# Attention scores of two layers in smaller TensorE tiles: layer 0 from 64x128 to 64x64, layer 3 from 32x128 to 32x64

## The chip, the cores and the metric

One core of a Trainium2 chip runs the whole program. The metric is the device time of one execution in microseconds (us); lower is better. A run is called faster or slower only beyond 2%. All runs told here were in the fast state.

A few names, as the profile uses them: PE is TensorE's matmuls, PEld its weight loads, ACT is ScalarE, DVE is VectorE. L1321 is line 1321 of that kernel; after an edit the same statement has another number. A tile of 32x128 (32\*128 in the profile) is a part of TensorE's array, 32 rows by 128 columns; several tiles work side by side as a pack (the first passes of layer 3's four start within 20 ns, and one record reads 640 ns), and the shape of the tile is the tile mode. A matmul in float32 leaves two records in the trace, its first and its second pass (the 1024 matmuls of L1008 leave 2048). A weight load is exposed when TensorE has nothing to stream meanwhile. In a group's row, what stands between the bars is its busy us and the mean ns of one record; after the second bar comes its engine's idle time before it and what ended that. A row of a timeline starts with its start and its length in us. A semaphore event is the record by which the trace tells that something another engine waits for is done.

## The reference, cut to what matters

Four layers work on x of 4 images, 64 x 64 tokens, 64 channels, all in float32. Layers 0, 2 and 3 are attentions; layer 1 is a convolution block with 1x1 projections.

```python
# layer 0: per image, 4096 tokens of 64 channels
energy = jnp.einsum('bic,bjc->bij', q, k)
attn = jax.nn.softmax(energy, axis=-1)
out = jnp.einsum('bmn,bmc->bnc', attn, v)
# ... layer 1 (convolution block), layer 2 (attention of 64x64) cut
# layer 3: per image, 4096 tokens of 32 channels
f = jnp.einsum('bnd,bmd->bnm', theta_x, phi_x)
f = jax.nn.softmax(f, axis=-1)
y = jnp.einsum('bnm,bmd->bnd', f, g_x)
```

## The kernel before

The scores are built in PSUM buffers called `ps` (128x1024 each, three buffers). ScalarE takes the exponential of a whole `ps` into an SBUF tile `e`, and TensorE multiplies `e` with the values. Scores of one step, products of an earlier step and, in layers 0 and 2, pieces of the convolution block are issued in a fixed order. That a matmul behind a waiting one waits too is what experiment 4 shows: there the second of a set starts 0.191 us after the first, because it waits, and the third 7 ns behind the second.

```python
def new_ps(name="ps"):                                  # pool of 3 buffers
    return pp.tile([128, 1024], F32, tag="ps", name=name)

# layer 0: contraction over 64 channels, two row tiles side by side
for g in range(4):
    ps = new_ps()
    for r in range(2):
        rows_ = slice(64 * r, 64 * r + 64)
        mm(ps[:, bass.ts(r, 512)], m.q[rows_, bass.ts(t, 128)],
           x[rows_, bass.ts(g, 512)], start=True, stop=True)
    act(es[g // 2][:, bass.ts(g % 2, 1024)], ps, AF.Exp, bias=SHIFT0,
        accum_out=zs[:, g : g + 1])

# a projection of the convolution block: the same shape, 64 rows and 128 columns
for s in range(2):
    mm(ps[:, bass.ts(s, 512)], pw1[64 * s : 64 * s + 64, bass.ts(r, 128)],
       tok(y, s, j), start=True, stop=True)

# layer 3: contraction over 32 channels, four row tiles, two ps for a step
e = es[n] = new_e()
tiles = [new_ps(), new_ps()]
for k in range(4):
    rows_ = slice(32 * k, 32 * k + 32)
    mm(tiles[k // 2][:, bass.ts(k % 2, 512)], m.ph[rows_, bass.ts(mc, 128)],
       m.th[rows_, bass.ts(nb, 512)], start=True, stop=True)
for kp in range(2):
    act(e[:, bass.ts(kp, 1024)], tiles[kp], AF.Exp)
# ... products of step n - 2 follow; in about every tenth step also sums by matmul
```

Of the kernel before, what the change touches and what calls it, by code (L numbers as in the profile page):

```python
# [691 lines left out]
def fast_path(ctx: ExitStack, tc: tile.TileContext, a: dict, out: bass.AP, bad):  # L692
# [18 lines left out]
    def new_ps(name="ps"):  # L711
        return pp.tile([128, 1024], F32, tag="ps", name=name)

    def new_acc(name="acc"):
        return pa.tile([128, 512], F32, tag="acc", name=name)

    def new_e(name="e"):
        return ep.tile([128, 2048], F32, tag="e", name=name)

    def new_t(name="t"):  # L720
        return tp.tile([128, 1024], F32, tag="t", name=name)
# [7 lines left out]
    mm = nc.tensor.matmul  # L729
# [73 lines left out]
    for nm in names128:  # L803
        r = flat[nm].shape[0] // 128
# [126 lines left out]
    def at(i, fn):  # L931
        due.setdefault(i, []).append(fn)
# [63 lines left out]
    def layer0(b):  # L996
        x, m, first = X[:, b], im[b], len(items)
        tiles = {}

        def scores(t):  # L1000
            es = [new_e() for _ in range(2)]
            zs = sm.tile([128, 4], F32, tag="zs", name="zs", bufs=4)
            vq = sm.tile([128, C], F32, tag="vq", name="vq", bufs=4)
            for g in range(4):
                ps = new_ps()
                for r in range(2):
                    rows_ = slice(64 * r, 64 * r + 64)
                    mm(  # L1008
                        ps[:, bass.ts(r, 512)], m.q[rows_, bass.ts(t, 128)],
                        x[rows_, bass.ts(g, 512)], start=True, stop=True,  # L1010
                    )
                act(  # L1012
                    es[g // 2][:, bass.ts(g % 2, 1024)], ps, AF.Exp, bias=SHIFT0,
                    accum_out=zs[:, g : g + 1],
                )
            tiles[t] = es, vq, zs

        def scale(t):
            es, vq, zs = tiles[t]
            tot = sums0[:, b, t : t + 1]  # L1020
            nc.vector.tensor_reduce(tot, zs, AX.X, ALU.add)
            rec = sm.tile([128, 1], F32, tag="rec", name="rec")
            nc.vector.reciprocal(rec, tot)
            nc.vector.tensor_scalar_mul(vq, m.v[:, t, :], rec)

        def products(p, half):
            accs = [new_acc() for _ in range(2)]
            for t in (2 * p, 2 * p + 1):
                es, vq, _ = tiles[t]
                for g in range(2):  # L1030
                    for r in range(2):
                        mm(  # L1032
                            accs[g][64 * r : 64 * r + 64, :], vq,
                            es[half][:, 1024 * g + 512 * r : 1024 * g + 512 * r + 512],
                            start=t == 2 * p, stop=t == 2 * p + 1,
                        )
            for g in range(2):
                cols = bass.ts(2 * half + g, 512)
                stt(  # L1039
                    (x if p == 15 else m.y)[:, cols], accs[g], gam0,  # L1040
                    (m.y if p else x)[:, cols], ALU.mult, ALU.add,
                )

        for t in range(32):
            items.append((lambda t=t: scores(t), 3.6))
        for p in range(16):
            for half in range(2):
                at(first + 2 * p + 2 + half, lambda p=p, half=half: products(p, half))
        for t in range(32):
            at(first + t, lambda t=t: scale(t))  # L1050
# [260 lines left out]
    def layer3(b):  # L1311
        m, first, last = im[b], len(items), b == B - 1
        es, st = {}, {}

        def scores(n):
            nb, mc = n // 32, n % 32
            e = es[n] = new_e()
            tiles = [new_ps(), new_ps()]
            for k in range(4):
                rows_ = slice(32 * k, 32 * k + 32)  # L1320
                mm(  # L1321
                    tiles[k // 2][:, bass.ts(k % 2, 512)], m.ph[rows_, bass.ts(mc, 128)],
                    m.th[rows_, bass.ts(nb, 512)], start=True, stop=True,
                )
            for kp in range(2):
                act(e[:, bass.ts(kp, 1024)], tiles[kp], AF.Exp)  # L1326

# [86 lines left out]
        for n in range(64):  # L1414
            items.append((lambda n=n: scores(n), 1.0))
            at(first + n + 2, lambda n=n: products(n))
            if last and n == 63:
                at(first + n + 2, close_last)
            elif n % 32 == 31:
                at(first + n + (2 if n == 63 and b < 2 else 4), lambda n=n: totals(n // 32))  # L1420
                at(first + n + 8, lambda n=n: close(n // 32))
# [69 lines left out]
    ps = new_ps()  # L1491
# [13 lines left out]
    for b in range(B):  # L1505
        dst = out[b].rearrange(by_rows, p=2, q=16)
        for g in range(2):
# [9 lines left out]
            ps = new_ps()  # L1517
# [23 lines left out]
    for i, (v, lo, hi) in enumerate(vals):  # L1541
        n = v.shape[1]
        total += 128 * n
        t = new_t("inside")
        nc.vector.tensor_scalar(t[:, 0:n], v, lo, None, ALU.is_ge)
        stt(t[:, 0:n], v, hi, t[:, 0:n], ALU.is_le, ALU.mult, accum_out=good[:, i : i + 1])
    ps = new_ps()
# [52 lines left out]
```

## Time and profile before

| | before |
|---|---|
| median of 3 runs (a fourth came with the result) | 2722.68 us (2719.42 to 2723.97) |
| span of the profiled run | 2718.6 us |
| granted TensorE clock | 0.994 |
| instructions in the trace | 41825 |
| layer 3, from its first to its last score group, three stretches | 146.8 + 146.6 + 304.3 = 597.7 us |

Layer 3's images 0 and 1 stand each in a stretch of their own, images 2 and 3 follow one another in the third. The lines that carry the reading are in the prediction below. Read them for one thing above all: a busy TensorE tells nothing about the short gaps in which it loads weights (534 against 429 ns from the first to the second pass in layer 0's scores) or changes its tile mode (519 against 422 ns from the last record of one group to the first of the next). For those one needs the starts of single records.

### The profile page before, as it was taken

Reading aid. Unit: us, or ns where it says so; the run is one execution under the profiler, and the core shown is the slowest. Engines: PE = TensorE matmul, PEld = TensorE weight load, DVE = VectorE, ACT = ScalarE, POOL = GpSimd, SP = SyncE. Lnnn points to the kernel's source line nnn. Section 1 sums busy time; section 2 is a strip of 40 time slices with the busy share of each in tenths; the row PEclk is TensorE's granted clock in tenths of the full one; section 3 lists DMA queues with packets and bytes.
Section 4 is the critical chain, followed back from the end, with each engine's and each line's share of the span. In section 5 each row is a group of like instructions: output and inputs, shape, how many; then the busy total and the mean of one; then the engine's idle time right before and its main releaser. Section 6 shows DMA issues by size and latency. Waiting matters only on the chain.

```text
span 2718.6 us, 41825 instructions
## 1 busy us (share of the span) xinstructions
PE 2656.8 (98%) x18042; PEld 902.6 (33%) x18042; DVE 1349.0 (50%) x1507; ACT 1724.6 (63%) x2796; POOL 16.6 (1%) x66
## 2 busy tenths in 40 slices
PE   8999999999999999999999999999999999999996
PEld 3343333333333333323333332243322333322222
DVE  3232478437773478216720027920058700088888
ACT  4545655565556555555655668855678756578886
POOL 2000000000000000000000000000000000000000
PEclk9999999999999999999999999999999999999998
DMA  3000000000000000000010000010000010010001
GB/s 71 0 1 1 1 1 1 1 1 1 1 1 1 8 8 1 1 1 17 1 32 1 16 1 1 1 32 1 17 1 1 1 32 1 1 32 1 1 1 64
DMA packets 17349, 24.33 MB, mean 9 GB/s; under 512 B 2460, under 2 KB 10885, under 8 KB 17157
## 3 DMA queue, kind: packets, MB, share of 16 engines
q1 hardware_dynamic: 16085, 20.47, 3.1%
q8 instruction: 143, 2.34, 0.4%
q0 software_dynamic: 672, 0.56, 0.1%
q10 hardware_dynamic: 400, 0.56, 0.1%
q14 instruction: 49, 0.40, 0.0%
HBM read 4.80 MB, written 4.19 MB: 3 GB/s over the span
## 4 chain that ended last, share of the span: by engine, by line
PE 94%; DVE 4%; ACT 2%; issue 0%; DMA 0%; ACTq 0%; DVEq 0%
PE acc L1032 17%; PE ps L1008 17%; PE acc L1224 16%; PE ps L1207 16%; PE ps L1321 11%; PE acc L1348 9%; PE ps L1103 1%; PE ps L1160 1%; PE accz L1337 1%; PE ps L1078 1%; PE ps L1143 1%; PE ps L1171 1%; PE ps L1064 1%; PE ps L1302 1%; PE ps L985 1%; DVE tg L1344 0%
## 5 line engine op out<-in xcount | busy, mean ns | idle before, releaser
L1012 ACT ACTIVATE e<-ps 128x1024 f32<-128x1024 f32 x512 | 517.1, 1024 | 343.4 <-PE ps L1008 231.0
L1215 ACT ACTIVATE e<-ps 128x1024 f32<-128x1024 f32 x512 | 517.1, 1024 | 308.1 <-PE ps L1207 308.0
L1326 ACT ACTIVATE e<-ps 128x1024 f32<-128x1024 f32 x512 | 495.4, 1022 | 94.9 <-PE ps L1321 85.1
L1344 DVE TENSOR_TENSOR tg<-tg,e 128x2048 f32<-128x2048 f32 x214 | 490.4, 2292 | 26.1 <-ACT e L1326 7.4
L1008 PE MATMUL ps<-X,q 64*128 64x512 f32 x2048 | 482.7, 608 | 11.3 <-ACT e L1012 4.2
L1207 PE MATMUL ps<-ko 64*64 64x512 f32 x4096 | 470.4, 593 | 7.8 <-ACT ko L1189 5.5
L1224 PE MATMUL acc<-e,X 64*64 64x512 f32 x4096 | 468.0, 591 | 2.7 <-DVE X L1039 2.1
L1032 PE MATMUL acc<-e,vq 128*64 128x512 f32 x2048 | 468.4, 599 | 0.0
L1321 PE MATMUL ps<-tg,ph 32*128 32x512 f32 x2048 | 321.2, 640 | 0.5 <-ACT e L1326 0.5
L1039 DVE SCALAR_TENSOR_TENSOR yv<-acc,gam,yv 128x512 f32<-128x512 f32 x224 | 168.0, 750 | 290.4 <-PE acc L1032 278.6
L1008 PEld LDWEIGHTS ps<-X,q 64*128 64x128 f32 x2048 | 187.0, 187 | 295.3 <-issue 190.1
L1348 PE MATMUL acc<-e,tg 128*32 128x512 f32 x2048 | 272.0, 603 | 1.3 <-ACT yz L1354 1.3
L1207 PEld LDWEIGHTS ps<-ko 64*64 64x64 f32 x4096 | 156.4, 133 | 294.7 <-issue 196.4
L1224 PEld LDWEIGHTS acc<-e,X 64*64 64x64 f32 x4096 | 159.6, 133 | 280.3 <-issue 265.0
L1032 PEld LDWEIGHTS acc<-e,vq 128*64 128x64 f32 x2048 | 136.6, 137 | 311.7 <-issue 290.3
L1232 DVE TENSOR_TENSOR ph<-ph,acc 128x512 f32<-128x512 f32 x16 | 11.0, 688 | 423.7 <-ACT ph L1231 423.7
L1321 PEld LDWEIGHTS ps<-tg,ph 32*128 32x128 f32 x2048 | 103.2, 182 | 219.2 <-issue 139.9
L1125 DVE SCALAR_TENSOR_TENSOR yg<-pad,vec,yg 128x1024 f32<-128x1024 f32 x128 | 164.3, 1283 | 5.9 <-ACT pad L1108 2.4
L1125 DVE SCALAR_TENSOR_TENSOR y<-pad,vec,y 128x1024 f32<-128x1024 f32 x128 | 164.3, 1284 | 3.7
L1348 PEld LDWEIGHTS acc<-e,tg 128*32 128x32 f32 x2048 | 43.5, 108 | 190.6 <-issue 185.1
L1215 ACT ACTIVATION_READ_ACCUMULATOR e<-ps 128x1 f32 x512 | 106.0, 207 | 0.0
L1012 ACT ACTIVATION_READ_ACCUMULATOR e<-ps 128x1 f32 x512 | 106.0, 207 | 0.0
(187 smaller groups left out, 996.5 us busy)
## 6 DMA issues: line engine op xcount, KB each, us to landing
ph<-tg SPq DMA_DIRECT2D x64, 128.0 KB
ko<-ko SPq DMA_DIRECT2D x16, 256.0 KB
out_dram<-o SPq DMA_DIRECT2D x8, 512.0 KB
xr<-in_x_dram SPq DMA_DIRECT2D x14, 256.0 KB
xr<-in_x_dram ACTq DMA_DIRECT2D x2, 256.0 KB
pw<-in_L_conv_pw_w_dram POOLq DMA_DIRECT2D x4, 64.0 KB, 4.6
sca<-in_L_conv_sca_w_dram POOLq DMA_DIRECT2D x1, 64.0 KB, 6.2
pw<-in_L_conv_pw_w_dram POOLq DMA_DIRECT2D x2, 32.0 KB, 4.8
```

Of the source, the lines that this page charges most:

```text
L1008: mm(ps[:, bass.ts(r, 512)], m.q[rows_, bass.ts(t, 128)], x[rows_, bass.ts(g, 512)], start=True, stop=True,)
L1012: act(es[g // 2][:, bass.ts(g % 2, 1024)], ps, AF.Exp, bias=SHIFT0, accum_out=zs[:, g : g + 1],)
L1032: mm(accs[g][64 * r : 64 * r + 64, :], vq, es[half][:, 1024 * g + 512 * r : 1024 * g + 512 * r + 512], start=t == 2 * p, stop=t == 2 * p + 1,)
L1039: stt((x if p == 15 else m.y)[:, cols], accs[g], gam0, (m.y if p else x)[:, cols], ALU.mult, ALU.add,)
L1125: stt(out_, win, wt, out_, ALU.mult, ALU.add)
L1207: mm(ps[64 * c : 64 * c + 64, bass.ts(r, 512)], m.ko[rows_, 128 * jb + 64 * c : 128 * jb + 64 * c + 64], m.ko[rows_, bass.ts(2 * ib + r, 5 ...
L1215: act(es[n, jb], ps, AF.Exp, bias=SHIFT2, accum_out=m.zs[:, jb, ib : ib + 1])
L1224: mm(acc[r][64 * c : 64 * c + 64, :], xw[rows_, jb, :], es[n, jb][rows_, bass.ts(c, 512)], start=jb == 0, stop=jb == 31,)
L1321: mm(tiles[k // 2][:, bass.ts(k % 2, 512)], m.ph[rows_, bass.ts(mc, 128)], m.th[rows_, bass.ts(nb, 512)], start=True, stop=True,)
L1326: act(e[:, bass.ts(kp, 1024)], tiles[kp], AF.Exp)
L1344: nc.vector.tensor_add(esum, esum, e)
L1348: mm(st["y"][32 * k : 32 * k + 32, :], m.gx[:, mc, :], e[:, bass.ts(k, 512)], start=mc == 0, stop=mc == 31,)
```

## The change

The intent: tiles of 64 columns instead of 128 load their weights faster (133 against 187 ns for a record; where the load is exposed, it costs 51 against 105 ns), so less of the load is exposed where it can't be hidden.

```diff
@@ layer 0
-                for r in range(2):
-                    rows_ = slice(64 * r, 64 * r + 64)
-                    mm(
-                        ps[:, bass.ts(r, 512)], m.q[rows_, bass.ts(t, 128)],
-                        x[rows_, bass.ts(g, 512)], start=True, stop=True,
-                    )
+                for c in range(2):
+                    for r in range(2):
+                        rows_ = slice(64 * r, 64 * r + 64)
+                        mm(
+                            ps[64 * c : 64 * c + 64, bass.ts(r, 512)],
+                            m.q[rows_, 128 * t + 64 * c : 128 * t + 64 * c + 64],
+                            x[rows_, bass.ts(g, 512)], start=True, stop=True,
+                        )
@@ layer 3
-            for k in range(4):
-                rows_ = slice(32 * k, 32 * k + 32)
-                mm(
-                    tiles[k // 2][:, bass.ts(k % 2, 512)], m.ph[rows_, bass.ts(mc, 128)],
-                    m.th[rows_, bass.ts(nb, 512)], start=True, stop=True,
-                )
+            for c in range(2):
+                for k in range(4):
+                    rows_ = slice(32 * k, 32 * k + 32)
+                    mm(
+                        tiles[k // 2][64 * c : 64 * c + 64, bass.ts(k % 2, 512)],
+                        m.ph[rows_, 128 * mc + 64 * c : 128 * mc + 64 * c + 64],
+                        m.th[rows_, bass.ts(nb, 512)], start=True, stop=True,
+                    )
```

## The prediction

Two measurements from the trace of the kernel before, to be kept in mind while reading: the matmuls of a pack start 6.7 ns apart (the four of a layer 3 set that doesn't wait at 0, 7, 13 and 20 ns), and in the 166 of layer 3's 256 score sets in which the third matmul waited, the fourth started 6 or 7 ns behind it.

> **What bounds the kernel now.** I read the page first, then the groups by line, then the timeline of a stretch of layer 3, then single records of the trace there. The page:
>
> ```profile
> PE 2656.8 (98%) x18042; PEld 902.6 (33%) x18042; DVE 1349.0 (50%) x1507; ACT 1724.6 (63%) x2796; POOL 16.6 (1%) x66
> ...
> PE 94%; DVE 4%; ACT 2%; issue 0%; DMA 0%; ACTq 0%; DVEq 0%
> PE acc L1032 17%; PE ps L1008 17%; PE acc L1224 16%; PE ps L1207 16%; PE ps L1321 11%; PE acc L1348 9%; PE ps L1103 1%; PE ps L1160 1%; PE accz L1337 1%; PE ps L1078 1%; PE ps L1143 1%; PE ps L1171 1%; PE ps L1064 1%; PE ps L1302 1%; PE ps L985 1%; DVE tg L1344 0%
> ```
>
> TensorE is busy 98% of the span and makes 94% of the chain that ended last. But busy is the union of overlapping records[...]. The chain's lines are the score and product matmuls of the three attention layers; the change touches L1008 (layer 0) and L1321 (layer 3). The groups:
>
> ```profile
> L1326 ACT ACTIVATE e<-ps 128x1024 f32<-128x1024 f32 x512 | 495.4, 1022 | 94.9 <-PE ps L1321 85.1
> ...
> L1008 PE MATMUL ps<-X,q 64*128 64x512 f32 x2048 | 482.7, 608 | 11.3 <-ACT e L1012 4.2
> L1207 PE MATMUL ps<-ko 64*64 64x512 f32 x4096 | 470.4, 593 | 7.8 <-ACT ko L1189 5.5
> L1321 PE MATMUL ps<-tg,ph 32*128 32x512 f32 x2048 | 321.2, 640 | 0.5 <-ACT e L1326 0.5
> ...
> L1008 PEld LDWEIGHTS ps<-X,q 64*128 64x128 f32 x2048 | 187.0, 187 | 295.3 <-issue 190.1
> L1207 PEld LDWEIGHTS ps<-ko 64*64 64x64 f32 x4096 | 156.4, 133 | 294.7 <-issue 196.4
> L1321 PEld LDWEIGHTS ps<-tg,ph 32*128 32x128 f32 x2048 | 103.2, 182 | 219.2 <-issue 139.9
> ```
>
> Each f32 matmul is two records (1024 instructions of L1008 give 2048). A load of 128 columns reads 187 ns, of 64 columns 133 ns. Layer 2 (L1207) already has the 64*64 tiles that layer 0 is to get. Now layer 3 in order of time, near its last image:
>
> ```profile
> 2592.80 0.37 PEld L1321 LDWEIGHTS ps<-tg,ph 32*128 32x128 f32 x8 [0.84 <-issue]
> 2592.80 1.20 PE L1321 MATMUL ps<-tg,ph 32*128 32x512 f32 x8
> 2593.93 0.16 PEld L1348 LDWEIGHTS acc<-e,tg 128*32 128x32 f32 x8 [0.76 <-issue]
> 2593.93 1.06 PE L1348 MATMUL acc<-e,tg 128*32 128x512 f32 x8
> 2593.97 1.94 ACT L1326 ACTIVATE e<-ps 128x1024 f32<-128x1024 f32 x2 [0.24 <-PE ps L1321]
> 2594.93 0.42 PEld L1321 LDWEIGHTS ps<-tg,ph 32*128 32x128 f32 x8 [0.84 <-issue]
> 2594.93 1.25 PE L1321 MATMUL ps<-tg,ph 32*128 32x512 f32 x8
> 2596.10 1.94 ACT L1326 ACTIVATE e<-ps 128x1024 f32<-128x1024 f32 x2 [0.19 <-PE ps L1321]
> 2596.11 0.16 PEld L1348 LDWEIGHTS acc<-e,tg 128*32 128x32 f32 x8 [0.76 <-issue]
> 2596.11 1.06 PE L1348 MATMUL acc<-e,tg 128*32 128x512 f32 x8
> 2597.10 0.37 PEld L1321 LDWEIGHTS ps<-tg,ph 32*128 32x128 f32 x8 [0.84 <-issue]
> ```
>
> One step of layer 3 is one group of scores, one of products and two exponentials. It starts at 2592.80, 2594.93, 2597.10: 2.13 and 2.17 us. ScalarE is busy 1.94 us of it, then waits about 0.2 us for the scores. So neither engine alone sets the pace: they pass it to and fro through the three `ps` buffers. That coupling is what the prediction turns on.
>
> [...] from the last record of one group to the first of the next is 517 to 523 ns whenever the mode changes (64*128 to 128*64, 64*64 to 128*64, 32*128 to 128*32, all alike) and 422 (two tiles) or 409 (four tiles) where it stays; about 97 ns a change. [...] a group whose weights could not be fetched during the one before it takes 534 ns from first to second pass with 128 columns, 480 with 64, against 429 in steady flow. So an exposed load costs 105 or 51 ns. [...] Here they start 6.7 ns apart, and a matmul that waits for a semaphore holds up all behind it. [...]
>
> **The change part by part.** Streaming time does not change: [...] The instructions double, their 429 ns per set of passes stays. Layer 2 shows four 64*64 tiles in 429 ns, layer 3's products four column tiles with four different moving streams. What changes is load exposure, mode changes and the order of instructions behind waits.
>
> Layer 0. In the records 153 sets of L1008 start with exposed weights (102 after another line, 50 after a wait inside the scores, and the first); each saves 54 ns: −8.3 us. But 64*128 is also the mode of the projections of the interleaved convolution (L1103, L1160, L975), so today scores and those share a mode. There are 26 boundaries from such a group to scores and 25 the other way. Each becomes a mode change: 26 × (97 + 51) = 3.8 us; of the 25, 13 now run without exposure, × (97 + 105) = 2.6 us, and 12 already do, × about 54 = 0.6 us. At about 127 exits the last of four tiles starts 13 ns later: 1.7 us. Sum −8.3 + 3.8 + 2.6 + 0.6 + 1.7 = +0.4 us. Layer 0 gains nothing. Each `ps` there still waits only ahead of its own first matmul.
>
> Layer 3, before. Let S be the start of the first `ps`'s scores, K of the second's, A of the first exponential. From the records: A = S + 0.542 + 0.635 (second pass of its last matmul, then its completion to ScalarE) = S + 1.177. The second `ps` of the next step is the buffer that this exponential frees: next K = A + 1.077 (1.02 plus the way back) = S + 2.254, if not held by TensorE. TensorE: next S = K + 0.542 + 0.518 (change) + 0.998 (products and change back) = K + 2.058. With k = K − S that gives next k = max(0.013, 0.196 − k): waits of two steps add to about 0.2 us, and the mean step is 2.058 + 0.098 = 2.156. The trace has just that: K − S reads 0.074, 0.126, 0.074, 0.126, and other stretches alternate 2.067 and 2.238 (mean 2.153).
>
> Layer 3, after. The loop puts the column half outside, so the order is two matmuls of the first `ps`, two of the second, then the other halves. The compiled order shows the wait for the second `ps` on the third of the eight, and the last two matmuls of the first `ps` behind it. The first exponential therefore now waits for K, not S: A = K + 0.020 + 0.480 + 0.635 = K + 1.135, and next K = A + 1.077 = K + 2.212. TensorE would need only K + 0.033 + 0.480 + 0.518 + 0.998 = K + 2.029, plus 0.013. So the saved 54 ns fall into a wait, and the loop buffer–exponential–buffer, closed in every step, sets 2.212 us. Of ten steps one also carries the sums by matmul (L1337, 0.858 us more), which absorbs the wait of that and of the following step. Before: 4 × (2.071 + 2.241) + 2.071 + 3.099 = 22.42 us. After: 3.070 + 2.042 + 8 × 2.212 = 22.81. That is +0.39 us in ten, and for 256 steps +10 us.
>
> Layers 1 and 2 and the ends are untouched. Sum: 2722.7 + 0.4 + 10 = 2733 us.
>
> **The rivals.** First, the 64-column load is a plain gain: if the wait on the third matmul didn't hold back the first `ps` (or its buffer were free by then), the step would fall from 2.154 to about 2.042 in some 230 steps: −26 us, giving 2697. Against it: the compiled order, and that the buffer is not free, as K − S above shows. VectorE with 2.29 us per sum in nine of ten steps (20.6 us of then 21.3) would just not stop it. Second, eight tiles might not run together: the only 32*64 group now, L1379, packs four, all in different rows, with 480 ns between passes. If two column tiles of one row strip ran in turn, a step would grow by two passes, 0.858 us: +220 us, 2940. Against it: column tiles with different streams run together in L1348 and L1224. For it: the early halves are now started up to 0.19 us apart, which no group of today shows. Third, layer 0 might gain all of its 8 us if new mode changes were cheap: 2725.
>
> **Range and chances.** I give my main path about 65%, the plain gain 20%, half-effects the rest except 6% for tiles that collide. So 2733, range 2699 to 2746. Faster by over 2% (below 2668) needs more than the whole exposed loading: 2%. Slower by over 2% (above 2777) needs the collision: 6%. Within 2%: 92%.
>
> **What would show it.** Right: steps of layer 3 of 2.21 us without alternation, 2.04 after a step with L1337; second `ps` starting about 0.18 us after the first; idle time ahead of L1326 up from 94.9 to about 110; 480 ns between passes in both score groups; 519 ns between L1103 and scores. Wrong: steps near 2.05 (plain gain), scores lasting nearly 2 us (collision), or mode changes missing at the projections.

## The result, and the profile after

| | before | after |
|---|---|---|
| median (4 runs each, same batch) | 2722.66 us | 2731.07 us (2730.07 to 2732.46) |
| span of the profiled run | 2718.6 us | 2728.9 us |
| instructions in the trace | 41825 | 50017 |
| layer 3, three stretches | 597.7 us | 150.6 + 150.3 + 310.5 = 611.4 us |

The ratio is 1.0033, with a 95% interval of 1.0016 to 1.0050. Ratios here are the mean time of one kernel's fast runs over that of the other's of the same batch, so not quite the ratio of the medians. A later batch gave 1.0048 (2732.74 against 2719.56 us; 1.0035 to 1.0062). So the change is a little slower, clear of noise, and "same" by the 2% rule.

The groups by line of the changed kernel, in the same form as before (L1330, L1009 and L1324 are what L1326, L1008 and L1321 were):

```profile
L1330 ACT ACTIVATE e<-ps 128x1024 f32<-128x1024 f32 x512 | 496.5, 1022 | 108.0 <-PE ps L1324 97.6
...
L1009 PE MATMUL ps<-X,q 64*64 64x512 f32 x4096 | 475.0, 599 | 11.2 <-ACT e L1014 4.4
...
L1324 PE MATMUL ps<-tg,ph 32*64 32x512 f32 x4096 | 336.0, 613 | 0.6 <-ACT e L1330 0.6
...
L1009 PEld LDWEIGHTS ps<-X,q 64*64 64x64 f32 x4096 | 141.5, 132 | 328.1 <-issue 221.0
...
L1324 PEld LDWEIGHTS ps<-tg,ph 32*64 32x64 f32 x4096 | 99.5, 129 | 224.2 <-issue 179.3
```

The loads did become shorter: 182 to 129 ns in layer 3, 187 to 132 in layer 0. Yet the score group of layer 3 is busy 336.0 us instead of 321.2, and ScalarE waits 108.0 us instead of 94.9 ahead of its exponentials. The timeline of layer 3, to be laid beside the one in the prediction:

```profile
2601.10 0.48 PEld L1324 LDWEIGHTS ps<-tg,ph 32*64 32x64 f32 x16 [0.84 <-issue]
2601.11 1.36 PE L1324 MATMUL ps<-tg,ph 32*64 32x512 f32 x16
2602.40 0.16 PEld L1352 LDWEIGHTS acc<-e,tg 128*32 128x32 f32 x8 [0.81 <-issue]
2602.40 1.06 PE L1352 MATMUL acc<-e,tg 128*32 128x512 f32 x8
2602.52 1.94 ACT L1330 ACTIVATE e<-ps 128x1024 f32<-128x1024 f32 x2 [0.29 <-PE ps L1324]
2603.40 0.42 PEld L1324 LDWEIGHTS ps<-tg,ph 32*64 32x64 f32 x16 [0.84 <-issue]
2603.40 1.30 PE L1324 MATMUL ps<-tg,ph 32*64 32x512 f32 x16
2604.63 0.16 PEld L1352 LDWEIGHTS acc<-e,tg 128*32 128x32 f32 x8 [0.81 <-issue]
2604.63 1.06 PE L1352 MATMUL acc<-e,tg 128*32 128x512 f32 x8
2604.75 1.94 ACT L1330 ACTIVATE e<-ps 128x1024 f32<-128x1024 f32 x2 [0.29 <-PE ps L1324]
2605.63 0.42 PEld L1324 LDWEIGHTS ps<-tg,ph 32*64 32x64 f32 x16 [0.84 <-issue]
```

The first step shown takes 2.30 us and is still disturbed; the next goes from 2603.40 to 2605.63, that is 2.23. Most undisturbed steps now read 2.231, where before they alternated between 2.067 and 2.238 (or 2.127 and 2.179), mean 2.153. The load row of one group lasts 0.42 us although a load lasts 0.13: it is stretched by the wait inside. ScalarE's idle time before each pair is 0.29 us and no longer alternates between 0.19 and 0.24.

Where the span's 10.3 us come from: layer 3's stretches 13.7 us longer; the stretch from the first to the last score of layer 0 2.9 us shorter (1049.7 against 1046.8); the remaining parts are each within 0.3 us. The 2.9 us are, as far as the clock records tell, not the change's doing. The trace's clock records have short spells of half clock (0.5; elsewhere in these two traces they show 1.0); within that stretch they add up to 13.6 us in the run before and 6.8 us in the one after. These are the two kernels at the same place, just behind a pause of TensorE of 1.6 us (columns of a row: window, its length, busy time of PE, PEld, DVE, ACT and POOL with counts, granted clock, DMA share, GB/s):

```profile
803.00:806.00 3.00, 3.00 (x10) 1.43 (x10) 0.69 (x1) 1.73 (x3) 0.00 (x0) 0.52 0.00 0
```

```profile
803.00:806.00 3.00, 3.00 (x32) 0.90 (x24) 0.69 (x1) 2.68 (x6) 0.00 (x0) 1.00 0.00 0
```

The first, of the kernel before, was granted half a clock (0.52) and the second, of the changed kernel, a full one, for the same scores. The spell at this pause lasts 3.4 us; the others in the stretch are one of 3.4 and one of 6.8 us before, and two of 3.4 us after. What starts a spell was not shown. Of the nine traces only that of the kernel before has a spell at this pause, so it is taken for chance. An estimate that takes off half of the half-clock time (13.6 and 6.8 us) leaves 1042.8 us before and 1043.4 after for layer 0: +0.5 us.

### The profile page after: what moved, and what is told of

The parts are those of the page before. It is cut to its first block, busy times and chain, and to the rows that moved or that the text cites. A ratio compares the mean times of both kernels' runs of the same rounds, so it can differ in the third digit from the quotient of the medians.

```text
span 2728.9 us, 50017 instructions
## 1 busy us (share of the span) xinstructions
PE 2668.4 (98%) x22138; PEld 852.0 (31%) x22138; DVE 1348.6 (49%) x1507; ACT 1725.6 (63%) x2796; POOL 16.8 (1%) x66
## 4 chain that ended last, share of the span: by engine, by line
PE 94%; DVE 4%; ACT 2%; issue 0%; DMA 0%; ACTq 0%; DVEq 0%
PE acc L1034 17%; PE ps L1009 16%; PE acc L1226 16%; PE ps L1209 16%; PE ps L1324 11%; PE acc L1352 9%; PE ps L1105 1%; PE ps L1162 1%; PE accz L1341 1%; PE ps L1080 1%; DVE tg L1348 1%; PE ps L1145 1%; PE ps L1173 1%; PE ps L1066 1%; PE ps L1304 1%; PE ps L985 1%
## 5 line engine op out<-in xcount | busy, mean ns | idle before, releaser
L1330 ACT ACTIVATE e<-ps 128x1024 f32<-128x1024 f32 x512 | 496.5, 1022 | 108.0 <-PE ps L1324 97.6
L1348 DVE TENSOR_TENSOR tg<-tg,e 128x2048 f32<-128x2048 f32 x214 | 490.4, 2292 | 30.1 <-ACT e L1330 11.4
L1009 PE MATMUL ps<-X,q 64*64 64x512 f32 x4096 | 475.0, 599 | 11.2 <-ACT e L1014 4.4
L1324 PE MATMUL ps<-tg,ph 32*64 32x512 f32 x4096 | 336.0, 613 | 0.6 <-ACT e L1330 0.6
L1009 PEld LDWEIGHTS ps<-X,q 64*64 64x64 f32 x4096 | 141.5, 132 | 328.1 <-issue 221.0
L1324 PEld LDWEIGHTS ps<-tg,ph 32*64 32x64 f32 x4096 | 99.5, 129 | 224.2 <-issue 179.3
```

Of the source, the lines that this page charges most:

```text
L1009: mm(ps[64 * c : 64 * c + 64, bass.ts(r, 512)], m.q[rows_, 128 * t + 64 * c : 128 * t + 64 * c + 64], x[rows_, bass.ts(g, 512)], start=Tru ...
L1324: mm(tiles[k // 2][64 * c : 64 * c + 64, bass.ts(k % 2, 512)], m.ph[rows_, 128 * mc + 64 * c : 128 * mc + 64 * c + 64], m.th[rows_, bass.t ...
L1348: nc.vector.tensor_add(esum, esum, e)
```

## The experiments

Seven kernels ran, five rounds each, in two batches; all gave correct results. Layer 0 alone has 13 runs on record, the third kernel of the table 6, the others 5. By the 2% rule all seven are "same"; what is told below are differences inside it that the intervals resolve. In the first batch the kernel before had a median of 2719.77 us, in the second 2719.56.

| kernel | median us | ratio (95%) | layer 3 us | layer 0 us, clock taken out |
|---|---|---|---|---|
| layer 0 alone | 2718.42 | 0.9994 (0.9986 to 1.0003) | 597.7 | 1042.6 |
| layer 3 alone | 2733.02 | 1.0050 (1.0036 to 1.0063) | 611.3 | 1043.3 |
| layer 3, first `ps` whole | 2711.39 | 0.9972 (0.9960 to 0.9984) | 590.3 | 1043.6 |
| layer 3, old tiles, mixed order | 2738.49 | 1.0069 (1.0055 to 1.0083) | 616.9 | 1043.7 |
| layer 0 and projections | 2707.78 | 0.9959 (0.9945 to 0.9973) | 597.7 | 1037.3 |
| layer 0, projections, layer 3 first `ps` whole | 2701.15 | 0.9934 (0.9920 to 0.9947) | 590.3 | 1037.7 |
| the changed kernel again | 2732.74 | 1.0048 (1.0035 to 1.0062) | 611.3 | 1043.2 |

The column for layer 0 is the time from the first to the last score record less half of the half-clock time in it, one profile each; runs with the same layer 0 differ by up to 0.9 us there. The column for layer 3 repeats within 0.1 us.

**1. Layer 0 alone.** The diff is the first hunk of the change.

> Layer 0 alone in 64x64 tiles, layer 3 as before. My theory (saved weight loads are paid back by new mode changes at the convolution's projections): ratio to before about 1.000, within 0.15% once the short half-clock windows are set aside; steps of layer 3 alternate 2.067 and 2.238 us again. Rival (the load saving in layer 0 is a real gain and the mode changes are cheap): 8 us faster, ratio 0.997, and the whole slowdown of the changed kernel then needs more than 17 us from layer 3.

Measured 0.9994, an interval that holds 1. Layer 3 is 597.7 us as before, with steps of 2066 and 2238 ns again. Over the runs with old scores layer 0 took 1042.8, 1043.3, 1043.6 and 1043.7 us, with new ones 1042.6, 1043.2 and 1043.4. Layer 0's part is nothing that these runs can tell from zero. The rival's 8 us are excluded.

**2. Layer 3 alone.** The diff is the second hunk.

> Layer 3 alone in 32x64 tiles with the changed kernel's order. My theory: all of the slowdown is here, 13.7 us from the first to the last steps of layer 3 as in the changed kernel, ratio 1.005, steps of 2.231 us without alternation. Rival (the slowdown comes from twice the instructions anywhere, or from layer 0): less than 5 us.

Measured 1.0050, and 611.3 us in layer 3: all of the slowdown is here.

**3. The new tiles with the first `ps` whole.** Only the order of the eight matmuls is changed against experiment 2; the first four now fill the first `ps`.

```diff
-            for c in range(2):
-                for k in range(4):
+            for k2, c, kk in [(i, j, l) for i in range(2) for j in range(2) for l in range(2)]:
+                k = 2 * k2 + kk
```

> Layer 3 in the same 32x64 tiles, but all four matmuls of the first ps ahead of the wait for the second; layer 0 as before. My theory (the order behind the wait costs, not the tiles): the first exponential no longer waits for the second ps; steps alternate about 2.04 and 2.20, mean 2.12, layer 3 some 8 us faster than before, ratio 0.997. Rival A (eight column tiles or doubled instructions cost by themselves): still 2.2 us a step, slower than before. Rival B (the exposed load was the whole story): steps of 2.04, 26 us faster.

Measured 0.9972, and 590.3 us in layer 3, 7.4 less than before. Two rows of its groups, and a stretch of its timeline:

```profile
L1328 ACT ACTIVATE e<-ps 128x1024 f32<-128x1024 f32 x512 | 495.4, 1022 | 87.5 <-PE ps L1322 79.2
...
L1322 PE MATMUL ps<-tg,ph 32*64 32x512 f32 x4096 | 313.5, 613 | 0.5 <-ACT e L1328 0.5
```

```profile
2589.97 0.34 PEld L1322 LDWEIGHTS ps<-tg,ph 32*64 32x64 f32 x16 [0.84 <-issue]
...
2591.13 1.94 ACT L1328 ACTIVATE e<-ps 128x1024 f32<-128x1024 f32 x2 [0.16 <-PE ps L1322]
2592.12 0.29 PEld L1322 LDWEIGHTS ps<-tg,ph 32*64 32x64 f32 x16 [0.84 <-issue]
...
2593.27 1.94 ACT L1328 ACTIVATE e<-ps 128x1024 f32<-128x1024 f32 x2 [0.21 <-PE ps L1322]
2594.22 0.34 PEld L1322 LDWEIGHTS ps<-tg,ph 32*64 32x64 f32 x16 [0.84 <-issue]
```

The alternation is back (2.15 and 2.10 us here, 2.040 and 2.205 elsewhere), and ScalarE's idle time falls to 87.5 us. The tiles, the sixteen records and the bytes are those of experiment 2; only the order differs, and it is worth 21 us. Rival A is out. Rival B is out too: the gain is 7.4 us and not 26, because the loop between TensorE and ScalarE still closes over every two steps: two together take 4.245 us however they are split, against 4.305 before.

**4. The old tiles with the order mixed.** Nothing of the change is in it but a first `ps` whose last matmul stands behind the second's wait.

```diff
-            for k in range(4):
+            for k in (0, 2, 1, 3):
```

> Layer 3 in the old 32x128 tiles, with the four matmuls in the order first ps, second, first, second; layer 0 as before. My theory: the last matmul of the first ps stands behind the wait, next K = K + 0.007 + 0.535 + 0.635 + 1.077, so each step is 2.254 us without alternation, layer 3 about 20 us longer than before, ratio 1.0075. Rival (the tiles cause the slowdown, the order doesn't matter): as before, ratio 1.000.

Measured 1.0069, 616.9 us in layer 3 (19.2 more), undisturbed steps of 2.251 or 2.252 us without alternation. In the records the second matmul, which waits, starts 0.191 us after the first, and the third, which is the last of the first `ps`, 7 ns behind the second. So the order makes the kernel slower without the new tiles, and the new tiles without the order make it faster. A stretch of its timeline:

```profile
2602.59 0.50 PEld L1321 LDWEIGHTS ps<-tg,ph 32*128 32x128 f32 x8 [0.84 <-issue]
...
2603.96 1.94 ACT L1326 ACTIVATE e<-ps 128x1024 f32<-128x1024 f32 x2 [0.31 <-PE ps L1321]
2604.84 0.50 PEld L1321 LDWEIGHTS ps<-tg,ph 32*128 32x128 f32 x8 [0.84 <-issue]
```

The load row has the same length in each step, 0.50 us, with the wait inside it; before it was 0.37 and 0.42 in turn.

**5. Layer 0 and the projections in 64x64.** If mode changes at the projections cost what layer 0 gains, the projections in the same tiles must bring it back. Shown is one of three edits of the same kind (L975, L1103, L1160), on top of the first hunk of the change.

```diff
-                    mm(
-                        ps[:, bass.ts(s, 512)], pw1[64 * s : 64 * s + 64, bass.ts(r, 128)],
-                        tok(y, s, j), start=True, stop=True,
-                    )
+                    for c in range(2):
+                        mm(
+                            ps[64 * c : 64 * c + 64, bass.ts(s, 512)],
+                            pw1[64 * s : 64 * s + 64, 128 * r + 64 * c : 128 * r + 64 * c + 64],
+                            tok(y, s, j), start=True, stop=True,
+                        )
```

> Layer 0 scores in 64x64, and the 64-row projections that are interleaved with layers 0 and 2 (L975, L1103, L1160) split into 64x64 tiles too; layer 3 as before. My theory (mode changes at these boundaries eat the load saving): 88 mode changes of about 97 ns go compared with layer 0 alone, and the load exposed at each (51 or 105 ns): 12 to 16 us faster than layer 0 alone, ratio to before about 0.995. Rival (mode changes don't cost, only exposed loads): 5 us at most.

Measured 0.9959. Layer 0 is 5 to 6 us shorter than in experiment 1, and the stretch from the first score of layer 2 to that of layer 3 is 5.5 us shorter than before (535.6 against 541.1, both with 6.8 us of half clock): together some 11 us, a little under the 12 to 16 expected and over the 5 of the rival. The mechanism shows in the records: up to 1600 us there are 378 changes of tile mode instead of 464, and from a projection to the scores it is 409 ns now where it was 519. Of these 110 ns 97 are the mode change and 13 the later start of the last of four tiles. Here is one projection and the scores behind it, before, in the changed kernel and in this one; the scores start 0.86, 0.96 and 0.86 us after the projection:

```profile
406.23 1.02 PE L975 MATMUL ps<-X,wq 64*128 64x512 f32 x4
407.09 3.73 PE L1008 MATMUL ps<-X,q 64*128 64x512 f32 x16
```

```profile
404.78 1.02 PE L975 MATMUL ps<-X,wq 64*128 64x512 f32 x4
405.74 3.66 PE L1009 MATMUL ps<-X,q 64*64 64x512 f32 x32
```

```profile
403.90 1.04 PE L976 MATMUL ps<-X,wq 64*64 64x512 f32 x8
404.76 3.72 PE L1011 MATMUL ps<-X,q 64*64 64x512 f32 x32
```

The size was overestimated: 86 changes at 97 ns are 8.3 us, so only about 3 us were saved on loads. At 11 of the boundaries from scores to a projection the next set waits for ScalarE anyway and starts after 505 ns.

**6. Both together.** Experiment 5 with layer 3 of experiment 3.

> The projections and layer 0 in 64x64 and layer 3 in 32x64 with the first ps whole ahead of the wait. My theory: the parts add up, about 14 us from the mode changes and 8 from layer 3, 22 us faster than before, ratio 0.992. Rival (gains of one part are lost again in the other's waits): no more than 14 us.

Measured 0.9934, 2701.15 us, 18 us faster than before and 32 faster than the change as it was made (both medians of the last batch are 2719.56 and 2732.74). The product of the two ratios of experiments 5 and 3 is 0.9931, so the parts add up. The 22 us were missed by what experiment 5 had already missed. This is the best version that ran.

**7. The changed kernel again.**

> The changed kernel once more on the chip of this batch, to compare with its parts: ratio about 1.003 to 1.005; in its trace the half-clock windows may lie elsewhere, the steps of layer 3 are 2.231 us again.

Measured 1.0048, layer 3 at 611.3 us, steps of 2231 ns; the half-clock spells lay elsewhere (one of 3.4 us in layer 0).

## Why the prediction was right

**Streaming time doesn't change: right.** Eight 32x64 tiles run together. In a set that didn't wait, the first passes start 6.7 ns apart and the second ones 0.480 us after the first. The second rival, tiles that collide, is out: a step would have taken an estimated 3 us (2.154 and two passes of 0.429), and most take 2.231.

**Layer 0 as a sum of small terms, +0.4 us: right as far as it can be seen.** A recount finds 148 of the 512 sets exposed and not 153, which is 0.3 us of the sum. Aligned record by record, 72 of the 80 stretches from a score group to the products after it became 36 to 41 ns shorter (54 of load less 14 of start skew), and in 25 of 26 cases the scores behind a projection start 519 ns after it instead of 422. So these two terms were confirmed. The sum of the profiled pair is +0.5 with the clock taken out; as kernels with the same layer 0 differ by up to 0.9 us, that it came so near to +0.4 can't be told from luck. Experiments 1 and 5 show both sides of the balance, with the size of the terms on the high side: experiment 5 was expected at 12 to 16 us and gave some 11.

**Layer 3 is set by the loop buffer, exponential, buffer, and the new order closes it in every step: right.** Experiments 3 and 4 show it crosswise. The alternation before had been read from the trace; its absence after, the step after one with L1337 (predicted 2.042, measured 2.040) and ScalarE's idle time (predicted about 110, measured 108.0) all came. The second `ps` starts 0.200 us after the first, predicted about 0.18.

**The size of layer 3's step was a little off.** Predicted 2.212 us, measured 2.231; predicted +10 us, measured +13.7. The term is "A = K + 0.020 + 0.480 + 0.635". The first two are right (0.500 measured from K to the second pass of the first `ps`'s last matmul). The third, from there to the start of the exponential, is 0.654 us in the changed kernel; the 0.635 was taken from the old one. The 19 ns in 206 steps (253 within the stretches, less 20 with L1337 and 27 of 2.040) are 3.9 us, about the 3.7 that were missed. The same difference stands between layers 0 of the two kernels (637 against 656 ns), and experiment 3 has 0.654 in its undisturbed loop too. The width of 64 columns alone doesn't make it. Already in the trace before, the semaphore that tells of the end is set 613 ns after the last second pass where two matmuls of 64x128 fill a buffer (L1008), 617 where two of 128x64 do (L1171), 633 where four of 64x64 do (L1207) and 637 where four of 128x32 do (L1348); for the first `ps` of layer 3 it is 612 before (two matmuls) and 632 after (four). So it goes with the number of matmuls more than with their width, and layer 2 already showed the right size of the term. Why it is so is open.

**That the total came so near is partly luck.** Predicted were +10.4 us; the medians of the first batch differ by 8.4, those of the later one by 13.2. Layer 3 was underestimated by 3.7 us, and in the profiled pair the half-clock spells took an estimated 3.4 us more from the kernel before.

**The first rival, the plain gain of 26 us: refuted,** by the changed kernel itself and by experiment 3, in which the third matmul's wait no longer holds back the first buffer and the gain is still 7.4 us only. **The third, 8 us in layer 0: refuted** by experiment 1.

## What to carry to other kernels

When a pack of matmuls fills several buffers, finish the first buffer before the first instruction that waits for the second: in experiment 4 the matmul behind a waiting one started 7 ns after it, and here an interleaving that looks free made the reader of the first buffer wait for the second one's release (611.3 us against 590.3 in layer 3, with the same tiles and the same instructions). Before counting a shorter weight load as a gain, write down the loop that sets the step (who frees which buffer for whom) and see whether the load is in it. And when one group's tile mode is changed, count its neighbours: here a change of mode took 97 ns from the last start to the next (519 against 422; 517 to 523 for all pairs of modes that the prediction names), plus the load that can then not be hidden, 105 ns for 128 columns and 51 for 64. Put all that are issued next to one another in the same mode; that was worth some 11 us in experiment 5.
